# A Fourier-layer tokenizer: the second spread of each image moved from chunk 0 to chunk 3, and one relu half moved from VectorE to ScalarE

## The chip, the cores and the metric

The kernel runs on one core of a Trainium2 chip. The metric is the device time of one execution in microseconds. A core has five engines that run their own instruction streams in order and wait for each other by semaphores: TensorE (matmuls; "PE" in the profile, its weight loads "PEld"), VectorE ("DVE"), ScalarE ("ACT"), GpSimd ("POOL") and SyncE ("SP", which here issues DMAs). Matmul results land in PSUM; VectorE and ScalarE empty it.

## The reference

64 images of 256 x 256 pass a tokenizer of four Fourier layers with 32 channels, then one transformer layer. In each Fourier layer (shortened):

```python
x_ft = jnp.fft.rfft2(v)
out1 = jnp.einsum('bixy,ioxy->boxy', x_ft[:, :, :M1, :M2], W1)
out2 = jnp.einsum('bixy,ioxy->boxy', x_ft[:, :, -M1:, :M2], W2)
...
x1 = jnp.fft.irfft2(out_ft, s=(Sx, Sy))
x2 = jnp.einsum('bcxy,cd->bdxy', v, w_w[i]) + w_b[i][None, :, None, None]
v = x1 + x2
v = (v - mean) * jax.lax.rsqrt(var + BN_EPS)
v = v * bn_g[i][None, :, None, None] + bn_b[i][None, :, None, None]
if i < L - 1:
    v = jax.nn.relu(v)
```

Only 24 x 12 modes are kept (M1 = M2 = 12), so the transforms are products with small tables of sines and cosines. After the fourth layer the channels are summed to one, 77 text tokens are appended, and attention and a token-selecting feed-forward follow. All data is float32.

## The kernel before, in words

The mixing of modes (`mix`) is a small stage before each layer. The bulk is `layer(i, ...)`, run for i = 0, 1, 2: it turns mixed modes back into an image, adds the 1 x 1 product of the layer's input, applies relu, writes the new image to DRAM, and in the same pass takes the modes of the new image for the next layer. Four calls of it matter here, each a step of an image b (of 64) or of a chunk t (of 8, one eighth of an image: 128 partitions x 2048 values, 1 MB):

- `spread(b, h)`: modes to half-transformed rows, for the half h of the image (chunks 0 to 3 need h = 0, chunks 4 to 7 need h = 1). Four matmul instructions (L598) into one PSUM tile, and a VectorE transpose (L602) into `y0` or `y1`, each of which exists once. It reads `ams[b % 2]`, the image's modes, which `load_am` (L567, two DMAs on SP) brings and `scale_am` (L586, GpSimd) scales.
- `pre(b, t)`: the layer's output for one chunk. Matmuls with `y` (L616, 16 instructions), and for i > 0 with the input chunk `vin` (L627, 32 instructions), into two PSUM tiles. Relu empties the first tile on ScalarE (L634) and the second on VectorE (L635) into `vo`, and SP issues the store (L636). In layer 0 the input image itself is in the operand `mv`, so there is no L627.
- `product(b, t)`: the next layer's 1 x 1 product of the chunk (L655), squared and summed on ScalarE (L662), for the batch statistics. `turn(b, t)`: a VectorE transpose of the chunk (L643, 2.3 us, after both relu halves).
- `along_y(b)` and `along_x(b)`: the modes of the finished image. `along_y` is 256 matmuls on the turned chunks (L672), its two PSUM tiles emptied by a ScalarE copy (L682) and two VectorE transposes (L684); `along_x` is 24 matmuls (L697), a ScalarE copy (L704) and a store.

PSUM is a ring ("ring" in the profile) of four tiles of two banks, taken in the order of the calls: `pre`, `product` and `along_y` take two tiles, `spread` and `along_x` one. A call waits until the tile four takings back is emptied.

The order of the work is the order in the program, for every engine; no scheduler changes it. In the loop (L718 on) chunk t of image b runs `pre(b, t)`, the load of the input chunk four ahead, `product` of the chunk before, then in some chunks a spread, then `turn(b, t)`. In chunks 1 and 2 the products are held back; at the end of chunk 2 comes `along_y(b - 1)` and then the two held products, and at the end of chunk 3 `along_x(b - 1)`. The modes' products of the previous image are thus made inside chunks 2 and 3 of the next. `spread(b, 1)` stands in chunk 0 with `load_am(b + 2)` behind it, `spread(b + 1, 0)` in chunk 5, `scale_am(b + 2)` in chunk 6. So the order on TensorE around the change is: pre(0), product(7 of the image before), spread(b, 1), pre(1), pre(2), along_y(b - 1), product(0), product(1), pre(3), product(2), along_x(b - 1), pre(4). On VectorE: relu(0), the spread's transpose, turn(0), relu(1), turn(1), relu(2), turn(2), the transposes of along_y, relu(3), turn(3), relu(4).

Of the kernel before, what the change touches and what calls it, by code (L numbers as in the profile page):

```python
# [10 lines left out]
AF = mybir.ActivationFunctionType  # L11
ALU = mybir.AluOpType
# [123 lines left out]
def tile_fno_fusion_transformer(ctx: ExitStack, tc: tile.TileContext, a, cst_d, grid_d, out):  # L136
    nc = tc.nc
    x = a["x"].rearrange("b x y o -> b x (y o)")
    B = x.shape[0]
# [368 lines left out]
    def layer(i, st, src, dst, acc):  # L508
# [7 lines left out]
        with ExitStack() as cx:  # L516
# [48 lines left out]
            def load_am(b):  # L565
                for n in range(2):
                    nc.sync.dma_start(  # L567
                        ams[b % 2][64 * n:64 * n + 2 * KX],
                        mix_d[i][b].rearrange("p k c -> (p k) c")[:, 512 * n:512 * n + 512],
                    )  # L570

            def load_x(b):
                for n in range(4):
                    nc.sync.dma_start(
                        mv[b % 2][32 * n + 24:32 * n + 28],
                        x[b].rearrange("(j n s) y -> n j s y", j=4, n=4)[n],
                    )

            def load_v(b, t):
                vin[b, t] = ip.tile([128, 8, S], F32, name="vin")  # L580
                nc.sync.dma_start(vin[b, t], src[b][:, t])

            def scale_am(b):
                for _, p0, cs in halves:
                    v = ams[b % 2][p0:p0 + 2 * KX].rearrange("p (c k) -> p c k", k=32)
                    nc.gpsimd.tensor_tensor(  # L586
                        v, v,
                        s_[p0:p0 + 2 * KX, cs].rearrange("p (c o) -> p c o", o=1)
                        .to_broadcast([2 * KX, 16, 32]), ALU.mult,
                    )  # L590

            def spread(b, h):

                y_[b, h] = yp.tile([128, 32, C], F32, name=f"y{h}")
                ps = pp.tile([128, 2, 512], F32, name="ring")
                for n in range(2):
                    hv = slice(64 * n, 64 * n + rows_)
                    nc.tensor.matmul(  # L598
                        ps[:, n, :], lhsT=EX[hv, 128 * h:128 * h + 128], rhs=ams[b % 2][hv],
                        start=True, stop=True, skip_group_check=True,  # L600
                    )
                nc.vector.transpose(  # L602
                    y_[b, h].rearrange("p q c -> p c q"), ps.rearrange("p n (c k) -> p (n c) k", k=32)
                )

            def four():

                t2 = [pp.tile([128, 2, 512], F32, name="ring") for _ in range(2)]
                return t2, [t2[n // 2][:, n % 2] for n in range(4)]

            def pre(b, t):
                t2, ps = four()
                for r in range(2):
                    for n in range(4):
                        q = 8 * (t % 4) + 4 * r
                        nc.tensor.matmul(  # L616
                            ps[n][:, 256 * r:256 * r + 256],
                            lhsT=y_[b, t // 4][32 * n:32 * n + K, q:q + 4, :].rearrange("p q c -> p (q c)"),
                            rhs=mv[b % 2][32 * n:32 * n + K, 2 * t + r, :] if i == 0 else T4[32 * n:32 * n + K, :],
                            start=r == 0, stop=i == 0, skip_group_check=True,  # L620
                        )
                if i:
                    v = vin.pop((b, t))
                    for k in range(4):
                        for n in range(4):
                            j = (n + k) % 4
                            nc.tensor.matmul(  # L627
                                ps[n][32 * j:32 * j + 32], lhsT=ws[32 * n:32 * n + 32],
                                rhs=v[32 * n:32 * n + 32, 2 * j:2 * j + 2, :], start=False, stop=True,
                                skip_group_check=True, tile_position=(32 * n, 32 * j),  # L630
                            )
                o = vo[b, t] = op.tile([128, 8, S], F32, name="vo")
                of = o.rearrange("p (n r) y -> p n (r y)", r=2)
                nc.scalar.activation(of[:, 0:2], t2[0], AF.Relu)  # L634
                nc.vector.tensor_scalar(of[:, 2:4], t2[1], 0.0, None, ALU.max)  # L635
                nc.sync.dma_start(dst[b][:, t], o)  # L636

            def turn(b, t):

                o = vo[b, t]  # L640
                if t % 2 == 0:
                    t32[b, t // 2] = tp.tile([128, 8, 16, C], F32, name="t32")
                nc.vector.transpose(  # L643
                    t32[b, t // 2][:, :, 8 * (t % 2):8 * (t % 2) + 8, :].rearrange("p y s c -> p s y c"),
                    o.rearrange("p s (y l) -> p s y l", l=32),
                )

            def product(b, t):

                o = vo.pop((b, t))  # L650
                t2, ps = four()
                for k in range(4):
                    for n in range(4):
                        j = (n + k) % 4
                        nc.tensor.matmul(  # L655
                            ps[n][32 * j:32 * j + 32], lhsT=w4[i + 1][32 * n:32 * n + 32],
                            rhs=o[32 * n:32 * n + 32, 2 * j:2 * j + 2, :], start=True, stop=True,
                            skip_group_check=True, tile_position=(32 * n, 32 * j),
                        )
                for n in range(2):  # L660
                    at = 2 * (8 * b + t) + n
                    nc.scalar.activation(t2[n], t2[n], AF.Square, accum_out=acc[:, at:at + 1])  # L662
# [3 lines left out]
            def along_y(b):  # L666
                t2, ps = four()
                for k in range(8):
                    for m in range(4):
                        for n in range(4):  # L670
                            j = (n + m) % 4
                            nc.tensor.matmul(  # L672
                                ps[n][32 * j:32 * j + 32], lhsT=FYT[32 * n:32 * n + 32, k, :],
                                rhs=t32[b, j][32 * n:32 * n + 32, k].rearrange("p s c -> p (s c)"),
                                start=k == 0, stop=k == 7, skip_group_check=True,
                                tile_position=(32 * n, 32 * j),
                            )
                for j in range(4):
                    t32.pop((b, j))
                zt = zts[b] = zp.tile([128, 2, 32, C], F32, name="zt")  # L680
                half = zp.tile([128, 2, 512], F32, name="half")
                nc.scalar.copy(half, t2[1])  # L682
                for h, s2 in enumerate((t2[0], half)):
                    nc.vector.transpose(  # L684
                        zt[:, h].rearrange("p k c -> p c k"),
                        s2.rearrange("p n (s c) -> p c (n s)", c=C),
                    )
# [29 lines left out]
            for b in range(B):  # L717
                for t in range(8):  # L718
                    pre(b, t)
                    nb, nt = (b, t + 4) if t < 4 else (b + 1, t - 4)  # L720
                    if i and nb < B:
                        load_v(nb, nt)
                    hold = b > 0 and t in (1, 2)
                    if not hold and (b or t):
                        product(*((b, t - 1) if t else (b - 1, 7)))
                    if t == 0:
                        spread(b, 1)
                        if b + 2 < B:
                            load_am(b + 2)
                    if t == 5 and b + 1 < B:  # L730
                        spread(b + 1, 0)
                    turn(b, t)
                    if hold and t == 2:

                        along_y(b - 1)
                        product(b, 0)
                        product(b, 1)
                    if b and t == 3:
                        along_x(b - 1)
                    if i == 0 and t == 0 and b + 1 < B:  # L740
                        load_x(b + 1)
                    if t == 6 and b + 2 < B:
                        scale_am(b + 2)
            product(B - 1, 7)
            along_y(B - 1)
# [409 lines left out]
```

## Time and profile before

| | |
|---|---|
| median of three runs | 12268.8 us (12255.74 to 12290.38) |
| the profiled execution | 12259.26 us, span of its instructions 12257.5 us |
| matmuls, busy | 11179.4 us, 91% of the span |
| VectorE busy | 8789.2 us, 72% |
| ScalarE busy | 6293.1 us, 51% |
| transposes of chunks (L643) | 1536 of 2302 ns |
| relu on VectorE (L635) | 1536 of 1206 ns |
| relu on ScalarE (L634) | 1536 of 1023 ns |
| squares on ScalarE (L662) | 3072 of 1012 ns |
| DMA rate inside layer 0 (400 to 2900 us) | 207 GB/s |
| DMA rate inside layer 1 (3200 to 6000 us) | 349 GB/s |

A line of the profile's table of groups names the line of the kernel, the engine, the operation, what it writes and reads (`out<-in`), and how often. In the timeline a line begins with the start and the duration in us; brackets give the engine's idle time before it and the instruction that ended that idle time. A waits line reads: engine and line that waited, what it waited for, total us, times, longest. Matmuls of small tiles overlap each other, so a group's matmul durations add up to more than its busy time. "issue" stands for idle time for which the profile shows no wait.

### The profile page before, as it was taken

The page shows a single profiled execution, that of the slowest core. Times are in us where ns is not written, and L with a number is a line of the kernel's source. Part 1 is how long each engine was busy: PE and PEld are TensorE (multiplying, and loading weights), DVE is VectorE, ACT ScalarE, POOL GpSimd, SP SyncE. Part 2 cuts the span into 40 slices and gives each one's busy share as a digit, 9 for nine tenths or more (in the row PEclk, how much of TensorE's full clock was granted, in tenths as well). Part 3 has the DMA queues.
Part 4 walks back from the last instruction along what each step waited for, and adds up shares of the span by engine and source line. Part 5 has one row for each costly group of instructions (what it writes and reads, how often), then busy time and mean ns, then how long its engine had stood idle before and what let it go on. Part 6 is the DMA issues. An engine that isn't in the chain of part 4 may idle for free. (4 is left out here: it accounts for less than half of the span.)

```text
span 12257.5 us, 405386 instructions
## 1 busy us (share of the span) xinstructions
PE 11179.4 (91%) x182038; PEld 5979.9 (49%) x182038; DVE 8789.2 (72%) x10661; ACT 6293.1 (51%) x10441; POOL 1326.8 (11%) x1987
## 2 busy tenths in 40 slices
PE   6999999997899999999969999999999699999998
PEld 3444444444444444444434444444444466666666
DVE  6888788776777777777767777777777566666665
ACT  5666565555555555555545555555555333333333
POOL 0000000001000000000010000000000133333333
PEclk7999999998899999999989999999999799999999
DMA  7555555556988999998889999999999755555553
GB/s 224 208 209 208 202 210 208 204 205 213 343 339 346 352 352 352 353 353 347 347 305 350 350 352 353 353 350 357 349 348 349 256 217 231 229 217 233 227 218 152
DMA packets 589288, 3485.10 MB, mean 284 GB/s; under 512 B 95001, under 2 KB 144537, under 8 KB 188569
## 3 DMA queue, kind: packets, MB, share of 16 engines
q1 hardware_dynamic: 539520, 3392.84, 71.9%
q0 software_dynamic: 40880, 62.59, 2.0%
q8 instruction: 1424, 23.33, 0.8%
q10 hardware_dynamic: 7144, 3.72, 0.1%
q14 instruction: 320, 2.61, 0.1%
HBM read 1761.87 MB, written 1696.92 MB: 282 GB/s over the span
## 5 line engine op out<-in xcount | busy, mean ns | idle before, releaser
L643 DVE STREAM_TRANSPOSE t<-vo 128x2048 f32<-128x2048 f32 x1536 | 3536.3, 2302 | 162.4 <-ACT vo L634 43.6
L662 ACT ACTIVATE ring<-ring 128x1024 f32<-128x1024 f32 x3072 | 3109.0, 1012 | 504.7 <-PE ring L655 434.7
L655 PE MATMUL ring<-vo,w 32*32 32x512 f32 x49152 | 2640.1, 623 | 80.4 <-issue 62.5
L635 DVE TENSOR_SCALAR vo<-ring 128x1024 f32<-128x1024 f32 x1536 | 1852.1, 1206 | 945.5 <-PE ring L627 739.3
L634 ACT ACTIVATE vo<-ring 128x1024 f32<-128x1024 f32 x1536 | 1570.6, 1023 | 1394.8 <-PE ring L627 1232.9
L672 PE MATMUL ring<-t,cst 32*32 32x512 f32 x49152 | 1996.4, 609 | 242.4 <-issue 171.2
L616 PE MATMUL ring<-cst,y 24*128 24x256 f32 x16384 | 1404.8, 405 | 171.5 <-DVE vo L635 150.8
L672 PEld LDWEIGHTS ring<-t,cst 32*32 32x32 f32 x49152 | 973.9, 103 | 1182.5 <-issue 661.4
L655 PEld LDWEIGHTS ring<-vo,w 32*32 32x32 f32 x49152 | 821.2, 105 | 1287.7 <-issue 656.6
L616 PEld LDWEIGHTS ring<-cst,y 24*128 24x128 f32 x16384 | 893.4, 185 | 1064.5 <-ACT vo L634 375.3
L586 POOL TENSOR_TENSOR ams<-ams,bns 48x512 f32<-48x512 f32 x384 | 400.8, 1044 | 8489.8 <-DMA ams<-mix 8309.5
L682 ACT COPY half<-ring 128x1024 f32<-128x1024 f32 x192 | 194.4, 1012 | 2014.1 <-PE ring L672 2014.1
L627 PE MATMUL ring<-vin,ws 32*32 32x512 f32 x32768 | 1219.7, 619 | 2.7 <-DMA vin<-v 2.7
L602 DVE STREAM_TRANSPOSE y<-ring 128x1024 f32<-128x1024 f32 x384 | 755.0, 1966 | 399.4 <-PE ring L598 399.4
L684 DVE STREAM_TRANSPOSE zt<-ring 128x1024 f32<-128x1024 f32 x192 | 374.0, 1948 | 827.8 <-PE ring L672 827.8
L616 PE MATMUL ring<-mv,y 29*128 29x256 f32 x8192 | 802.6, 421 | 133.0 <-DVE vo L635 121.4
L616 PEld LDWEIGHTS ring<-mv,y 29*128 29x128 f32 x8192 | 503.2, 193 | 598.5 <-DVE vo L635 247.2
L697 PEld LDWEIGHTS ring<-cst,zt 128*128 128x128 f32 x4608 | 535.3, 193 | 179.0 <-ACT vo L634 164.8
L662 ACT ACTIVATION_READ_ACCUMULATOR ring<-ring 128x1 f32 x3072 | 583.4, 190 | 0.0
L1104 POOL DMA_DIRECT2D out_dram<-o x1024 | 504.4, 501 | 656.2 <-DVE o L1099 627.3
L697 PE MATMUL ring<-cst,zt 128*128 128x96 f32 x4608 | 567.4, 280 | 8.7 <-DVE zt L684 8.7
L598 PE MATMUL ring<-ams,cst 49*128 49x512 f32 (+1 forms) x1536 | 457.6, 650 | 38.2 <-POOL ams L586 28.8
(366 smaller groups left out, 9638.6 us busy)
## 6 DMA issues: line engine op xcount, KB each, us to landing
v<-vo SPq DMA_DIRECT2D x1536, 1024.0 KB
vin<-v SPq DMA_DIRECT2D x1024, 1024.0 KB
ch<-v SPq DMA_DIRECT2D x512, 1024.0 KB
mix<-ob SPq DMA_DIRECT2D x96, 512.0 KB
ams<-mix SPq DMA_DIRECT2D x384, 96.0 KB
xin<-in_x_dram SPq DMA_DIRECT2D x16, 1024.0 KB
mv<-in_x_dram SPq DMA_DIRECT2D x256, 64.0 KB
out_dram<-o POOLq DMA_DIRECT2D x1024, 16.0 KB, 3.0
```

Of the source, the lines that this page charges most:

```text
L598: nc.tensor.matmul(ps[:, n, :], lhsT=EX[hv, 128 * h:128 * h + 128], rhs=ams[b % 2][hv], start=True, stop=True, skip_group_check=True,)
L602: nc.vector.transpose(y_[b, h].rearrange("p q c -> p c q"), ps.rearrange("p n (c k) -> p (n c) k", k=32))
L616: nc.tensor.matmul(ps[n][:, 256 * r:256 * r + 256], lhsT=y_[b, t // 4][32 * n:32 * n + K, q:q + 4, :].rearrange("p q c -> p (q c)"), rhs=m ...
L627: nc.tensor.matmul(ps[n][32 * j:32 * j + 32], lhsT=ws[32 * n:32 * n + 32], rhs=v[32 * n:32 * n + 32, 2 * j:2 * j + 2, :], start=False, sto ...
L634: nc.scalar.activation(of[:, 0:2], t2[0], AF.Relu)
L635: nc.vector.tensor_scalar(of[:, 2:4], t2[1], 0.0, None, ALU.max)
L643: nc.vector.transpose(t32[b, t // 2][:, :, 8 * (t % 2):8 * (t % 2) + 8, :].rearrange("p y s c -> p s y c"), o.rearrange("p s (y l) -> p s ...
L655: nc.tensor.matmul(ps[n][32 * j:32 * j + 32], lhsT=w4[i + 1][32 * n:32 * n + 32], rhs=o[32 * n:32 * n + 32, 2 * j:2 * j + 2, :], start=Tru ...
L662: nc.scalar.activation(t2[n], t2[n], AF.Square, accum_out=acc[:, at:at + 1])
L672: nc.tensor.matmul(ps[n][32 * j:32 * j + 32], lhsT=FYT[32 * n:32 * n + 32, k, :], rhs=t32[b, j][32 * n:32 * n + 32, k].rearrange("p s c -> ...
L697: nc.tensor.matmul(ps[:, 0, 96 * g:96 * g + 96], lhsT=zt[:, h, k0:k0 + 4, :].rearrange("p k c -> p (k c)"), rhs=FX[:, h, 48 * r:48 * r + 9 ...
L1104: nc.gpsimd.dma_start(out[b, 64 * n + 16 * g:64 * n + 16 * g + 16].rearrange("(p t) d -> p t d", t=2), o[32 * g + 8 * n:32 * g + 8 * n + 8 ...
```

## The change

Three edits in `layer`. The relu of the second PSUM tile goes to ScalarE in chunk 6 of every image, and in layer 0 in chunk 1 too; all other chunks keep VectorE. `spread(b, 1)`, and `load_am(b + 2)` with it, move from chunk 0 to chunk 3, where the spread stands after product(2) and ahead of turn(3) and `along_x(b - 1)`. `scale_am(b + 2)` moves from chunk 6 to chunk 7.

```diff
                 nc.scalar.activation(of[:, 0:2], t2[0], AF.Relu)
-                nc.vector.tensor_scalar(of[:, 2:4], t2[1], 0.0, None, ALU.max)
+
+                if t == 6 or i == 0 and t == 1:
+                    nc.scalar.activation(of[:, 2:4], t2[1], AF.Relu)
+                else:
+                    nc.vector.tensor_scalar(of[:, 2:4], t2[1], 0.0, None, ALU.max)
                 nc.sync.dma_start(dst[b][:, t], o)
...
-                    if t == 0:
+                    if t == 3:
                         spread(b, 1)
                         if b + 2 < B:
                             load_am(b + 2)
...
-                    if t == 6 and b + 2 < B:
+                    if t == 7 and b + 2 < B:
                         scale_am(b + 2)
```

After it the order on TensorE around that place is: pre(0), product(7 of the image before), pre(1), pre(2), along_y(b - 1), product(0), product(1), pre(3), product(2), spread(b, 1), along_x(b - 1), pre(4).

## The prediction

> **What bounds the kernel now.** The page first, for the engines and the slices:
>
> ```profile
> PE 11179.4 (91%) x182038; PEld 5979.9 (49%) x182038; DVE 8789.2 (72%) x10661; ACT 6293.1 (51%) x10441; POOL 1326.8 (11%) x1987
> ...
> DMA  7555555556988999998889999999999755555553
> ```
>
> Slices 1 to 9 are layer 0, 10 to 19 layer 1, 20 to 30 layer 2; the rest is the attention part, which the edit leaves alone. In windows inside each layer TensorE is busy for 92 to 93% (2309.66 of 2500 us, 2611.52 of 2800, 2709.14 of 2900), with DMA at 0.55 in layer 0 and 0.91 in layers 1 and 2. So the gaps of TensorE are what can be won. Who makes them is in its waits, asked for 400 to 2900 us (layer 0, 57 images by its 57 half copies, about 43.9 us each); columns are total us, times, longest:
>
> ```profile
> PE ring L616 <- DVE vo L635: 110.8, 114, 1.5
> PE ring L672 <- DVE vo L635: 63.9, 57, 1.1
> ...
> PE ring L655 <- issue: 1.7, 5, 0.7
> ```
>
> and for 3200 to 6000 us (layer 1, again 57 images, 49.1 us each; layer 2 looks the same):
>
> ```profile
> PE ring L672 <- issue: 79.1, 59, 2.6
> PE ring L616 <- DVE vo L635: 67.2, 57, 1.4
> PE ring L655 <- issue: 25.8, 19, 2.0
> ```
>
> TensorE waits for VectorE's half of the relu at pre (L616), twice an image in layer 0 and once in layer 1, and at along_y (L672); in layer 1 the latter shows in the weight loads, 44.4 us in 57. The timeline of one image of layer 1 says which chunks. VectorE:
>
> ```profile
> 5411.84 1.98 DVE L602 STREAM_TRANSPOSE y<-ring 128x1024 f32<-128x1024 f32 x1 [1.00 <-PE ring L598]
> 5413.66 2.29 DVE L643 STREAM_TRANSPOSE t<-vo 128x2048 f32<-128x2048 f32 x1
> 5415.86 1.20 DVE L635 TENSOR_SCALAR vo<-ring 128x1024 f32<-128x1024 f32 x1
> ```
>
> This is chunks 0 and 1: the transpose of the second spread (whose matmuls began at 5410.64), turn(0), relu(1); and along_y's main part waits until 5417.11 for that relu. TensorE, at chunk 7:
>
> ```profile
> 5451.19 0.70 PE L616 MATMUL ring<-cst,y 24*128 24x256 f32 x4
> 5453.11 1.13 PE L616 MATMUL ring<-cst,y 24*128 24x256 f32 x12 [1.22 <-DVE vo L635]
> ```
>
> Pre(7) stops after 4 of its 16 matmuls: the second pair of banks of pre(6) is emptied by relu(6) on VectorE, at 5451.86 to 5453.05, behind the transpose of spread(b+1, 0) and turn(5). In layer 0 both places are worse, as VectorE has no gap from chunk 5 to chunk 2 of the next image. VectorE, and then TensorE:
>
> ```profile
> 1844.59 1.92 DVE L602 STREAM_TRANSPOSE y<-ring 128x1024 f32<-128x1024 f32 x1
> 1846.38 2.25 DVE L643 STREAM_TRANSPOSE t<-vo 128x2048 f32<-128x2048 f32 x1
> 1848.57 1.17 DVE L635 TENSOR_SCALAR vo<-ring 128x1024 f32<-128x1024 f32 x1
> ```
>
> ```profile
> 1837.67 1.13 PE L616 MATMUL ring<-mv,y 29*128 29x256 f32 x12 [1.46 <-DVE vo L635]
> ...
> 1847.63 1.05 PE L672 MATMUL ring<-t,cst 32*32 32x512 f32 x4
> 1849.80 0.72 PE L672 MATMUL ring<-t,cst 32*32 32x512 f32 x16 [1.12 <-DVE vo L635]
> ```
>
> [...] pre(7) has the gap in all 57 images, and it waits for a PSUM buffer. [...] 1.02 us at L634 against 1.21 at L635. [...] where the two "issue" rows make 105/57 = 1.84 us per image. That this is fetching beside a full DMA is my reading, not shown.
>
> **The change part by part**, as times of the images above.
>
> *Chunk 6, layers 1 and 2.* ScalarE ends relu(6)'s first half at 5451.13 and is next busy with product(5)'s square, at 5451.23; the second half goes between, 1.02 us, to 5452.15. Pre(7)'s twelve start some 0.06 later, 5452.2 instead of 5453.11: 0.91 won, 0.33 of the gap stays. Behind it on ScalarE the two squares of product(5) slide by 0.92, the second to 5454.2; product(6), which needs those banks, itself now comes at 5454.15, so this costs about nothing (0.1 at most). VectorE loses 1.2 us of work, so turn(6) starts at 5452.2 and relu(7) meets pre(7)'s new end. 0.91 x 128 images = 116 us.
>
> *Spread, layers 1 and 2.* Without it pre(1) starts where the spread did, 5410.64: its banks are now pre(0)'s (the ring moves by one), emptied by ScalarE at 5410.59 and by VectorE at 5410.85, 0.5 before the matmuls get to them. Pre(1) behind a product takes 2.21 (7636.21 to 7638.42) and pre(2) 1.97 (7643.25 to 7645.22), so along_y begins at 5414.8, its main part 0.14 later, 5414.96. VectorE: turn(0) from 5410.91, relu(1) from 5413.2 to 5414.4: in time. Main part before 5417.11, so 2.15 won. At chunk 3 the spread's 1.06 (5410.64 to 5411.70) is paid between product(2) and along_x. Its bank is free with the relu(3) that along_x waits for now. Its transpose (1.2 after its matmuls start, 1.97 long) ends some 3.2 after that start; pre(4), which needs it, comes after spread and along_x, 1.06 + 2.84 = 3.9. A cover of 0.7 us: were it gone, pre(4) would wait by as much. Turn(3) is late by 2.7 behind that transpose and relu(4) would meet it just free (turn(3) before 5436.82 to 5439.1, relu(4) at 5441.79 plus 1.06). So net 2.15 - 1.06 = 1.09, say 1.0, in the 63 images a layer that have an along_y inside: 126 us.
>
> *Layer 0*, from one along_y's end (1816.09) on. Up to product(2) nothing changes. The spread starts at 1822.69 (where along_x did), its transpose at 1823.9, turn(3) at 1825.7 instead of 1822.52, relu(4) at 1827.95 instead of 1826.78, and from there VectorE and TensorE are late by 1.06 to 1.15. Then spread(b+1, 0)'s transpose at 1833.5, turn(5) at 1835.3, and no relu(6): turn(6) at 1837.5 instead of 1837.72, relu(7) at 1839.73, turn(7) 1841.02, relu(0) 1843.26 to 1844.44. ScalarE does relu(6)'s halves from 1834.6 to 1836.6, ahead of the squares of product(5), whose matmuls now end at 1836.6. No transpose of the spread stands here now; pre(1)'s second half follows relu(0) at 1844.5 and ends at 1845.6; ScalarE empties both its halves by 1847.7 (two of 1.02; on VectorE it would have been about 1848), and along_y's main part starts at 1847.8 instead of 1849.80. 2.0 us x 63 = 126 us. What was won twice (1.46 + 1.12 and the matmuls of the spread) is mostly paid back at chunk 3.
>
> *At nothing:* load_am, two issues of together 1.0 us on SP, moves with the spread. On SP it now waits for the spread of chunk 3 with along_x's store, store(4) and load(4) behind it, all of which are made later anyway. In layer 1 the load took from 5411.87 to the scaling at 5423.78, 12 us; it is needed at chunk 5 of the next image, over 40 us on. Scaling one chunk later is POOL's 2.16 us in 46 idle ones. With that cover gone the spread would stop TensorE by up to 12 us. Store 6 now waits for ScalarE alone, and earlier.
>
> *What may come back.* Layers 1 and 2 move the same bytes in 2 us less. The peak rate in a 25 us slice there is 413 GB/s against a mean of 350, so I don't take DMA as a bound. But the "issue" waits should grow; between 0 and 1.9 us (all of the gain) I take 0.3 per image, 16% of 1.84: 38 us.
>
> Sum: 116 + 126 + 126 - 38 = 330 us. Span 12257.5 - 330 = 11927.5; the profiled execution took 12259.3 (1.8 around the span), which lies 9.5 below the median of 12268.8. Against that median: about 11940.
>
> **Rivals.** (1) *Only layer 0 wins.* The waits for VectorE in layers 1 and 2 turn into waits for instructions or for loads, at 9 tenths DMA. For it: 1.84 us of issue waits there, next to none in layer 0. Against: loads are waited for only 36 us in all (weight loads at L627), and rates go to 413. 12268.8 - 126 = 12143. (2) *Slower, by the instruction stream.* TensorE's pauses at pre(7) and along_y are when its stream catches up; without them along_y and the products behind it run dry in each image. This decides where the issue waits grow by more than the gross gain, 368 us over 126 images, 2.9 us, to 4.8 us per image; at 5.5 (three times now) it is 3.66 x 126 = 461 lost, 12268.8 - 368 + 461 = 12362. Against: the longest single one is 2.6 us. (3) *Spread's move is even.* If pre(4) waits for the transpose by 1 us or more, all the move's gain in layers 1 and 2 is gone and half of layer 0's: 116 + 63 = 179, 12090.
>
> **How the numbers follow.** The forecast has 0.70, with a range of its own of 11860 (no issue growth, which gives 38 more, and 0.3 us more per image where the steps above were read a little too dear, another 42 or so) to 12030. Rival 3 has 0.10, rival 1 0.11, rival 2 0.05, and 0.04 is for a wash. The range 11860 to 12145 takes in all of forecast, 3 and 1 but tails, a little over 8 in 10. 0.3%, about 37 us, is what a measurement of this kernel tells from no change: faster 0.91, same 0.04, slower 0.05.
>
> **What would show it.** Right: no TensorE wait for L635 at along_y in any layer; the wait of pre(7) about 0.3 us and put down to ScalarE's new line; image period about 47.5 us in layers 1 and 2 and 42 in layer 0; VectorE's relu count down by 192 + 64 = 256 of 1536. Wrong: a wait of pre(4) for the spread's transpose (rival 3), "issue" rows well over 2.2 us per image (1, 2), waits for vin or stores, or a lower granted clock: 1% of it is some 84 us of TensorE's 373 in 400 over the layers.

## The result, and the profile after

The changed kernel takes 11956.81 us (median of four, 11949.38 to 11968.81) against 12273.2 us before (median of four): a ratio of 0.9743 (95% interval 0.9726 to 0.976), 316 us less. Forecast were 11940 and about 330 less. The total is right; its parts are not: two errors of opposite sign hide in it, and that they nearly cancel is luck. The page of the profiled execution (11961.02 us):

```profile
PE 11022.9 (92%) x182038; PEld 5966.9 (50%) x182038; DVE 8507.8 (71%) x10405; ACT 6492.7 (54%) x10697; POOL 1327.1 (11%) x1987
```

VectorE has 256 instructions fewer and ScalarE 256 more, as counted. The table that tells more is by layer. It is from the half copies of the modes (L682 before, L686 after), one per image: the time from the first to the last of a layer, 63 images, and in layer 0 the shortest image (the first and the last left out).

| | layer 0 | shortest image | layer 1 | layer 2 |
|---|---|---|---|---|
| before | 2742.8 us | 42.06 | 3087.3 | 3068.2 |
| changed | 2559.5 (-183) | 40.12 | 3019.7 (-68) | 3023.2 (-45) |
| forecast of the change | -126 | -2.0 | about -102 | about -102 |

Layer 0 gave more than forecast, layers 1 and 2 half. TensorE's waits in layer 1, asked for the same stretch as before the change, 3200 to 6000 us (58 images):

```profile
PE ring L676 <- issue: 102.3, 83, 4.4
PE ring L627 <- DMA vin<-v: 27.6, 38, 1.6
PE ring L659 <- issue: 26.9, 22, 1.8
PE ring L616 <- ACT vo L637: 12.4, 58, 0.2
```

Every wait for VectorE's relu is gone, at pre and at along_y. So it is in layer 0, where the longest sums from 400 to 2700 us are short waits for ScalarE's squares, in 57 images:

```profile
PE ring L616 <- ACT ring L666: 20.0, 62, 0.3
PE ring L659 <- ACT ring L666: 16.1, 58, 0.6
```

What is left at pre(7) in layer 1 is 0.21 us an image for ScalarE's new line (0.33 forecast). But "issue" at along_y, 79.1 us before, is 102.3, and there is a wait for input chunks, 0.48 us an image, that was not there. (Line numbers from L635 on are shifted by the edit: L655, L672 and L635 before are L659, L676 and L639 now.)

The step with the thin cover, chunk 3, in one image of layer 1; TensorE, then VectorE:

```profile
4436.82 1.13 PE L598 MATMUL ring<-ams,cst 49*128 49x512 f32 x4
4437.87 2.92 PE L701 MATMUL ring<-cst,zt 128*128 128x96 f32 x24
4440.72 1.15 PE L616 MATMUL ring<-cst,y 24*128 24x256 f32 x16
```

```profile
4438.02 1.97 DVE L602 STREAM_TRANSPOSE y<-ring 128x1024 f32<-128x1024 f32 x1 [0.99 <-PE ring L598]
```

The spread's transpose ends at 4439.99, and pre(4) starts at 4440.72 without a wait: 0.73 us of cover, 0.7 in the forecast. Rival 3 is out.

### The profile page after: what moved, and what is told of

It reads as the page before. It is cut to its first block, busy times and chain, and to the rows that moved or that the text cites. A ratio compares the mean times of both kernels' runs of the same rounds, so it can differ in the third digit from the quotient of the medians.

```text
span 11959.2 us, 405306 instructions
## 1 busy us (share of the span) xinstructions
PE 11022.9 (92%) x182038; PEld 5966.9 (50%) x182038; DVE 8507.8 (71%) x10405; ACT 6492.7 (54%) x10697; POOL 1327.1 (11%) x1987
## 5 line engine op out<-in xcount | busy, mean ns | idle before, releaser
L659 PE MATMUL ring<-vo,w 32*32 32x512 f32 x49152 | 2671.7, 603 | 97.6 <-issue 61.4
L676 PE MATMUL ring<-t,cst 32*32 32x512 f32 x49152 | 1868.1, 599 | 224.6 <-issue 223.9
L639 DVE TENSOR_SCALAR vo<-ring 128x1024 f32<-128x1024 f32 x1280 | 1550.0, 1211 | 611.4 <-PE ring L627 523.2
L676 PEld LDWEIGHTS ring<-t,cst 32*32 32x32 f32 x49152 | 981.9, 103 | 1036.4 <-issue 648.1
L659 PEld LDWEIGHTS ring<-vo,w 32*32 32x32 f32 x49152 | 823.0, 103 | 1348.0 <-issue 612.6
L686 ACT COPY half<-ring 128x1024 f32<-128x1024 f32 x192 | 194.3, 1012 | 1812.9 <-PE ring L676 1812.9
L616 PE MATMUL ring<-mv,y 29*128 29x256 f32 x8192 | 746.2, 408 | 44.1 <-ACT ring L666 22.0
L616 PEld LDWEIGHTS ring<-mv,y 29*128 29x128 f32 x8192 | 465.9, 185 | 474.4 <-ACT vo L634 167.2
```

What stands on the lines that cost most here:

```text
L616: nc.tensor.matmul(ps[n][:, 256 * r:256 * r + 256], lhsT=y_[b, t // 4][32 * n:32 * n + K, q:q + 4, :].rearrange("p q c -> p (q c)"), rhs=m ...
L659: nc.tensor.matmul(ps[n][32 * j:32 * j + 32], lhsT=w4[i + 1][32 * n:32 * n + 32], rhs=o[32 * n:32 * n + 32, 2 * j:2 * j + 2, :], start=Tru ...
L676: nc.tensor.matmul(ps[n][32 * j:32 * j + 32], lhsT=FYT[32 * n:32 * n + 32, k, :], rhs=t32[b, j][32 * n:32 * n + 32, k].rearrange("p s c -> ...
```

## The experiments

On the two edits there were two theories. A: the walk through VectorE's queue that the forecast made. B: each edit wins its own wait and the two add up. On what took the gain back in layers 1 and 2, D: DMA traffic; E: nothing was there to win; and, after the first runs, F: TensorE uses up its instructions faster than they arrive, and a pause lets them catch up.

### One edit at a time

The relu edits alone:

```diff
-                    if t == 3:
+                    if t == 0:
                         spread(b, 1)
...
-                    if t == 7 and b + 2 < B:
+                    if t == 6 and b + 2 < B:
```

> The kernel before with the relu halves of chunk 6 (all layers) and chunk 1 (layer 0) on ScalarE; the spread and its loads stay at chunk 0. Theory A, by the steps of the prediction: in layer 0 VectorE is the bound from chunk 5 to along_y, and each relu half taken from it is a gain of 1.2 to 1.3 us there. Relu(6) gone brings turn(6) to relu(0) forward by 1.29, relu(1) gone takes turn(0) and relu(1) out of along_y's way: its main part at about 1846.8 in the image of the forecast against 1849.80, 3.0 us, more than the 2.0 of the whole change, as nothing is paid at chunk 3. In layers 1 and 2 0.9 an image before what DMA takes back, half of it after. 190 + 60 = 250 us, 12020; if TensorE's clock in layer 0 rises with it as in the whole change, another 50, 11970. Theory B, each edit wins its own wait and they add up: the relu edits bring about half of the whole change, 150 to 170 us, 12110.

The move of the spread alone:

```diff
-                if t == 6 or i == 0 and t == 1:
-                    nc.scalar.activation(of[:, 2:4], t2[1], AF.Relu)
-                else:
-                    nc.vector.tensor_scalar(of[:, 2:4], t2[1], 0.0, None, ALU.max)
+                nc.vector.tensor_scalar(of[:, 2:4], t2[1], 0.0, None, ALU.max)
```

> The kernel before with the second spread and its loads at chunk 3 and the scaling at chunk 7; all relu halves of the second tile stay on VectorE. Theory A: in layer 0 relu(6) still stands in the VectorE queue, so that along_y's main part comes at 1849.3 instead of 1849.80 in the image of the forecast, 0.5 us, 32 us in all; in layers 1 and 2 1.0 an image before what DMA takes back, half of it after, 63 us. Together about 95 us, 12180, and the wait of pre(7) for VectorE is still there in every layer. Theory B, the edits add up: 150 us, 12120.

The whole change without chunk 1:

```diff
-                if t == 6 or i == 0 and t == 1:
+                if t == 6:
```

> The changed kernel without its chunk 1 edit: in layer 0 relu(1)'s second half is on VectorE again. Theory A: with the spread gone from chunk 0, VectorE reaches relu(1) at about the time at which ScalarE would do it as its second relu; along_y's main part is late by 0.2 to 0.3 us, 13 to 19 us in all, 11972, nothing in layers 1 and 2. Theory B, the chunk 1 edit is what took the wait of 1.12 us out of along_y in layer 0: 70 us slower, 12027.

| | median us | ratio to before | layer 0 | shortest image | layer 1 | layer 2 |
|---|---|---|---|---|---|---|
| relu edits alone | 11859.27 | 0.967 (0.9655 to 0.9685) | 2504.6 (-238) | 39.10 | 3015.8 (-72) | 2994.7 (-74) |
| spread's move alone | 12207.87 | 0.9958 (0.9941 to 0.9974) | 2660.3 (-83) | 41.58 | 3087.7 (0) | 3087.3 (+19) |
| change without chunk 1 | 11964.52 | 0.9754 (0.9739 to 0.9768) | 2564.0 (-179) | 40.23 | 3020.9 (-66) | 3018.9 (-49) |

The relu edits alone are faster than the whole change: the intervals of their ratios do not touch. Once they are made, the move of the spread costs 98 us by the medians (105 against the change without chunk 1, measured beside them): 55 in layer 0, 4 in layer 1 and 29 in layer 2 by the table. Theory B is out.

In layer 0 the walk of theory A holds. For one image it said 3.0 us for the relu edits, 0.5 for the move, 2.0 for both; between the shortest images 2.96, 0.48 and 1.94 are measured. For the whole layer the relu edits' 238 us are its 190 and the 50 that it allowed for TensorE's clock (0.97 before, 1.00 with them). The move's 83 are more than its 32: the rest comes from the slower images, as the mean image was 1.48 us above the shortest before and 0.65 with the move, at a mean clock (below) of 0.97 and 0.96; why is open. The move takes a transpose out of VectorE's busiest stretch, but pays for it at chunk 3, where VectorE has work behind it too; after the relu edits the transpose at chunk 0 no longer stands in along_y's way. Chunk 1's edit is worth 4 us in the layer and 8 by the medians, too little to be told from nothing.

In layers 1 and 2 theory A fails. It let half of the relu edits' gain there be taken back, and none was: their total came 110 us or more below its 11970 to 12020. And it fails for the move, which was to win 1.0 us an image before DMA. TensorE's waits of the kernel with the move alone, 3200 to 6000 us (57 images):

```profile
PE ring L673 <- issue: 116.9, 91, 2.0
PE ring L616 <- DVE vo L636: 66.9, 56, 1.3
PE ring L656 <- issue: 26.5, 19, 2.0
PE ring L627 <- DMA vin<-v: 5.6, 18, 0.6
```

Per image of layer 1 (3200 to 5800 us, by the half copies in it; the wait at along_y is that of its weight loads), in us:

| | relu at pre(7) | VectorE's relu at along_y | issue | vin |
|---|---|---|---|---|
| before | 1.15 | 0.78 | 1.87 | 0 |
| spread's move alone | 1.18 | 0 | 2.57 | 0.09 |
| relu edits alone | 0.21 | 0.76 | 1.94 | 0.04 |
| changed | 0.21 | 0 | 2.26 | 0.48 |

The move removes the wait at along_y, 0.78, and gets 0.70 of issue and 0.09 of vin in its place: the sum stays to 0.01. Once the relu edits are made it is the same: the move removes 0.76, and gets 0.32 of issue and 0.44 of vin. Of the wait at pre(7), which the relu edits remove, next to nothing comes back.

### Is it DMA? Half of the loads

Layers 1 and 2 load only four of the eight rows of each input chunk, in the kernel before, in each edit alone and in the whole change:

```diff
-                vin[b, t] = ip.tile([128, 8, S], F32, name="vin")
-                nc.sync.dma_start(vin[b, t], src[b][:, t])
+                vin[b, t] = ip.tile([128, 4, S], F32, name="vin")
+                nc.sync.dma_start(vin[b, t], src[b][:, t, 0:4])
...
-                                rhs=v[32 * n:32 * n + 32, 2 * j:2 * j + 2, :], start=False, stop=True,
+                                rhs=v[32 * n:32 * n + 32, 2 * (j % 2):2 * (j % 2) + 2, :], start=False, stop=True,
```

> The kernel before with half of each input chunk of layers 1 and 2 loaded: four of the eight rows, which the products then use twice; everything else as before. A quarter of those layers' DMA bytes is gone (what is computed from the rows left out is not the reference's). Theory D, the issue waits of layers 1 and 2 (1.84 us an image) come from DMA: they go down to some 0.3, each of the two layers is faster by 80 to 100 us, 12080 in all. Theory E, they come with the program, whatever the DMA does: the layers stay within 20 us each.

> The same half loads, with the spread and its loads at chunk 3 and no relu half moved. Against the half-load kernel before: theory D, it was DMA that took the gain of this move in layers 1 and 2 (with full loads 0 us in layer 1 and 19 us lost in layer 2): now the move brings its 1.0 us an image, 63 us in each layer, beside 83 in layer 0, 210 us in all. Theory E, the move brings nothing in these layers in any case: 80 us in all, from layer 0.

> The same half loads, with only the relu halves of chunk 6, and of chunk 1 in layer 0, on ScalarE. Against the half-load kernel before: 238 us in layer 0 as with full loads, and in each of layers 1 and 2 0.9 to 1.15 us an image, 57 to 72: 350 to 380 us in all, by both theories.

> The same half loads in the changed kernel. Against the half-load kernel before: 183 us in layer 0; theory D, in layers 1 and 2 the two edits now add up, 1.9 to 2.1 us an image or 120 to 130 in each, 430 us in all, faster than the relu edits alone by some 60; theory E, 70 in each, 320 us in all, slower than the relu edits alone by 50.

| half loads | median us | layer 1 | layer 2 | issue in layer 1, us an image |
|---|---|---|---|---|
| kernel before | 12117.36 | 3033.3 | 2999.0 | 1.25 |
| spread's move alone | 12209.61 | 3056.5 (+23) | 3092.0 (+93) | 2.22 |
| relu edits alone | 11697.6 | 2926.3 (-107) | 2922.8 (-76) | 1.23 |
| changed | 11909.08 | 2996.1 (-37) | 2980.8 (-18) | 2.50 |

The medians are of three, six, two and two runs. The layers' columns are of the profiled executions; that of the first row was 40 us above its median and that of the second 36 below, so that the move's loss is rather larger than these columns say. TensorE's first wait for instructions in layer 1, 3200 to 5800 us, in the half-load kernel before (54 images) and with the move (53):

```profile
PE ring L672 <- issue: 47.0, 34, 2.9
```

```profile
PE ring L673 <- issue: 112.1, 77, 2.8
```

The DMA share in layer 1 falls from 0.91 to 0.75 in the kernel before, and the issue waits from 1.87 to 1.25 us an image. The move of the spread does not win its microsecond here either. It loses: the whole kernel is 92 us slower by the medians, where theory D had said 210 faster and E 80, and issue grows by 0.97 us an image. Nor do the two edits add up: the whole change brings 208 us (D said 430, E 320) and is 212 behind the relu edits alone, which bring 420 (350 to 380 forecast).

What this does not show is that DMA has no part in it. The traffic is not gone where the waits stand. In an image of layer 1 with half loads and the move, along_y begins at 4393.71, and TensorE waits in it for 2.16 us until 4399.44. Stretches of 4 us up to there (busy us of PE, PEld, DVE, ACT, POOL, then granted clock, DMA share, GB/s):

```profile
4390.00:4394.00 4.00, 4.00 (x102) 1.84 (x100) 3.84 (x3) 2.54 (x5) 0.00 (x0) 1.00 1.02 402
4394.00:4398.00 4.00, 3.29 (x96) 1.61 (x93) 3.89 (x3) 1.02 (x1) 0.00 (x0) 1.00 1.00 394
4398.00:4402.00 4.00, 2.56 (x82) 1.41 (x97) 1.18 (x1) 0.00 (x0) 0.00 (x0) 1.00 1.01 414
```

The DMA is as full there as with whole loads; the mean share of 0.73 for this kernel's layer 1 hides that. So the half loads do not decide between the theories.

### Issue waits: traffic or instructions?

First, layer 0 of the changed kernel with the DMA traffic of the others:

```diff
+            junk_d = [dram.tile([128, 8 * S], F32, name=f"junk{n}") for n in range(8)] if i == 0 else None
...
+                    if i == 0:
+                        nc.sync.dma_start(junk_d[t], grid_d[:, 0:8 * S])
```

> The changed kernel with a copy of 1 MB from DRAM to DRAM added per chunk in layer 0, which nothing waits for; layer 0 then moves about what layers 1 and 2 do. Theory D, issue waits come with DMA traffic: in layer 0 they rise from 0.1 us an image to 1 or more. Theory F, they need a dense stream of instructions first, and layer 0 has 96 matmul and weight instructions a chunk against 160: they stay below 0.4.

Measured: 12321.59 us, layer 0 at 2870.1, 311 us longer. The DMA share there is 0.98, more than in any layer of the kernel, and issue waits are 12.0 us in 50 images, 0.24 an image, where the changed kernel has 0.04. What TensorE waits for is ScalarE's relu, whose own wait is the output buffer's store. ScalarE's waits, 400 to 2700 us:

```profile
ACT vo L635 <- DMA v<-vo: 355.3, 151, 4.5
```

So in this run a DMA at 0.98 did not by itself make long issue waits. The pauses that the stores make may have let instructions catch up, though, so this is not a clean test.

Second, fewer instructions on TensorE in layers 1 and 2, with the spread at chunk 0 and at chunk 3:

```diff
-                    for k in range(4):
-                        for n in range(4):
-                            j = (n + k) % 4
-                            nc.tensor.matmul(
-                                ps[n][32 * j:32 * j + 32], lhsT=ws[32 * n:32 * n + 32],
-                                rhs=v[32 * n:32 * n + 32, 2 * j:2 * j + 2, :], start=False, stop=True,
-                                skip_group_check=True, tile_position=(32 * n, 32 * j),
-                            )
+                    for n in range(4):
+                        nc.tensor.matmul(
+                            ps[n], lhsT=ID, rhs=v[:, 2 * n:2 * n + 2, :], start=False, stop=True,
+                            skip_group_check=True,
+                        )
```

> The kernel before with the 1 x 1 product of layers 1 and 2 inside pre made by four wide matmuls with the identity instead of sixteen of 32 x 32 with the weights (so that product is left out; its place in the order and about its time stay): 16 instructions a chunk on TensorE in place of 64. Theory F, TensorE runs through its instructions faster than they come before and in along_y, which is what its issue waits are: with 384 fewer an image they go from 1.86 us an image to 0.5 or less. Theory D, it is DMA traffic alone that delays them: they stay between 1.5 and 2.2.

> The same with the spread and its loads at chunk 3, no relu half moved. Against the kernel of the wide matmuls with the spread at chunk 0: theory F, with instructions to spare the move now brings its 1.0 us an image in layers 1 and 2, 63 us in each, and issue waits do not grow by more than 0.2 us; if loads come late as in the changed kernel some of it is lost to vin, 40 in each at the least. Theory E, the move brings nothing in layers 1 and 2 in any case: within 20 us in each.

This pair did not test what it was made for. The four wide matmuls took 3.63 us to the next group where the sixteen packed ones take 0.88, so the kernels run at 14218.63 and 14128.4 us and an image of layer 1 takes 64 us. At that pace hardly any wait for VectorE is left for the move to win, and it changed layer 1 by 4 us (4035.4 to 4031.2). Issue was 0.88 us an image without the move and 0.85 with it (35.3 us in 40 images, 35.0 in 41): it did not grow. That agrees with F; it does not show it.

The traces show it, without a further run. The profile's table of DMA queues has one for instructions, whose packets are 16 KB each (23.33 MB in 1424 before). In the kernel before, and with the wide matmuls (queue, kind: packets, MB, share of 16 engines):

```profile
q8 instruction: 1424, 23.33, 0.8%
```

```profile
q8 instruction: 1232, 20.19, 0.6%
```

The wide kernel has 384 fewer instructions on TensorE in each of 128 images, 49152, and 192 packets fewer. So this is TensorE's queue, and a packet is a block of 256 (49152/192) of its instructions. The whole count agrees: 182038 matmuls and as many weight loads before are 1422.2 blocks of 256. The trace has the start and the length of each packet. In the fourteen traces TensorE has 2673 issue waits inside the three layers. Counted through all of TensorE's instructions in a trace, every one of them stands at the same place of a block of 256 (number 193 or 194), and every one ends 1.1 to 1.8 us after the end of a packet of this queue. An along_y of layer 1 with the move alone:

```profile
4398.70 3.58 PE L673 MATMUL ring<-t,cst 32*32 32x512 f32 x96
4403.80 4.46 PE L673 MATMUL ring<-t,cst 32*32 32x512 f32 x128 [1.52 <-issue]
4410.01 1.15 PE L673 MATMUL ring<-t,cst 32*32 32x512 f32 x32 [1.75 <-issue]
```

Between the two waits lie 128 matmuls, with their weight loads 256 instructions; the packets went from 4401.38 to 4402.30 and from 4407.69 to 4408.66. An issue wait of TensorE in these layers is thus a wait for the next block of its own instructions, as theory F had it.

DMA traffic makes the block late in these runs, so theory D has its part. A packet takes about 1 us (medians of 0.94 to 1.06) whatever the traffic, but it starts later. From TensorE's first instruction of one block to the start of the packet for the next, the median is 0.94 us in layer 0 and 3.33 in layer 1 of the kernel before, and 1.85 with half loads; in layer 0 of the changed kernel the added copies raise it from 0.95 to 2.66. Of the 75 issue waits from 3200 to 5800 us before, 74 stand where the DMA share around the block's start was 0.95 or more, as it was for 294 of the 383 blocks; with half loads and the move, 80 of 83, where it was so for 189 of 388.

This fits with one gain kept and the other not. In the image above it is 6.21 us from TensorE's first instruction of a block to that of the next: 3.89 to the start of the packet, 0.97 for the packet, 1.35 until TensorE goes on. The median over all blocks of layer 1 that end in an issue wait is 6.21 too, before and with the move alone. TensorE's own work in this block is 4.46. A pause in such a block is time in which the next one arrives. In the kernel before, only 5 of the 62 blocks of layer 1 in which along_y's weight loads wait for VectorE's relu end in an issue wait. Without that pause more blocks do: of 106 that begin in along_y (3200 to 5800 us), TensorE waits for 55 before and for 85 with the move alone. The blocks around pre and product last longer by themselves: with the relu edits alone 7.0 us (median) for those whose successor begins in pre, and only 5 of these 159 successors are waited for, against 56 of 110 in along_y. So the wait at pre(7) could be won. This is read from the traces; no run was made to test it.

### The load ahead of the store

In the changed kernel, then with the relu edits alone:

```diff
-                nc.sync.dma_start(dst[b][:, t], o)
...
                     if i and nb < B:
                         load_v(nb, nt)
+                    nc.sync.dma_start(dst[b][:, t], vo[b, t])
```

> The changed kernel with each chunk's load of the input four ahead issued before the store of the chunk, on the same queue, instead of behind it; nothing else. Theory A: in layers 1 and 2 part of the gain was taken back by loads that now come late (TensorE at L627 waits for vin 0.48 us an image, 0.03 before). The store waits for relu, the load for matmuls that end about 1.1 us sooner, and it no longer runs behind the store's 1 MB (2.6 us at 400 GB/s): the load lands 3 us earlier and the wait goes, 0.45 x 126 = 57 us, 11900. Theory C, the loads' wait is only where a DMA queue that is full shows, and the bytes take their time anyway: within 0.3% of the changed kernel, the wait moves to instructions (issue) or stores.

> The relu edits alone, the spread left at chunk 0, and each chunk's load issued before its store. With the spread at chunk 0 the loads were not waited for, so most of what the earlier load won in the changed kernel (78 us) is not there to win: 11859 less 0 to 30 us, 11830 to 11860. If it is the order of stores and loads itself that helps, 11790.

In the changed kernel: 11878.3 us (ratio 0.9687, 0.9672 to 0.9701), 78.5 us less than the changed kernel; layers 1 and 2 at 2989.5 and 2975.1, the wait for vin gone, layer 0 unmoved. Theory A was right on this wait; it had forecast 57 us. With the relu edits alone: 11802.21 us (ratio 0.9629, 0.9611 to 0.9647), 57 us below those edits without it, between the two expectations. There the loads were hardly waited for (0.04 us an image), so only part of it is that wait; issue waits fall too, from 1.94 to 1.63 us an image of layer 1. What the rest is stays open. This version is the fastest of all that load every row, 155 us below the changed kernel.

## Why the prediction was right, and where its parts were wrong

**Chunk 6, layers 1 and 2: 116 forecast, 145 measured** (72 + 74 with the relu edits alone). The mechanism is as told: a gap of 1.15 us an image at pre(7) becomes 0.21. ScalarE's second relu starts 0.92 us after its first, not 1.02, which is 0.1 of the 1.14 us an image. The rest of the difference to 0.91 stays open; TensorE's clock in layer 1 was 0.98 before and 0.99 with the relu edits alone.

**The spread, layers 1 and 2: 126 forecast, 38 of it lost; measured a loss of 19** (0 in layer 1). This is the step that failed. The wait at along_y was removed as said, though it was 0.78 us an image in the mean, less than the 1.0 that was taken from one image; that TensorE would then run on into along_y without another wait was wrong. With the move alone issue waits grew by 0.70 us an image where 0.3 were put in; with the whole change they grew by 0.39, near the 0.3, but vin waits came to 0.48 where none was expected. What stood in the way is the next block of TensorE's instructions, which, where it is waited for, comes 6.2 us (median) after the one before: the pause that was removed had been the time in which it arrived. The prediction's reading of the issue waits, fetching beside a full DMA, was the right one; its sum did not follow from it, as it took the DMA for no bound because of its mean rate. In the kernel before, TensorE waited for 6 of 279 packets in layer 0 (400 to 2700 us) and for 75 of 383 in layer 1 (3200 to 5800 us).

**Loads are not a bound.** Wrong by 0.48 us an image: of the 36 us of waits before, all but 2.7 were in weight loads that hid behind matmuls, but the load of chunk 2, issued behind the store of chunk 6, had no slack. In the image shown of the changed kernel it is issued at 4405.57 and awaited until 4416.32.

**Layer 0: 126 forecast, 183 measured.** The walk was good to 0.06 us for the shortest image (1.94 against 2.0). For the mean of the images that ran at full clock (20 of 61 before, 60 of 61 after; the first and the last left out) it is 42.37 less 40.64, 1.73 us, or 109 in 63 images. What came on top is a term that the sum had only as a risk: TensorE's clock. From 400 to 2700 us its mean was 0.97 before and 1.00 after. Stretches of 2 us around the wait of pre(7), 1490.2 to 1491.7, in a slow image of the kernel before (busy us of PE, PEld, DVE, ACT, POOL, then granted clock, DMA share, GB/s):

```profile
1488.00:1490.00 2.00, 2.00 (x36) 0.53 (x32) 2.00 (x2) 0.79 (x2) 0.00 (x0) 1.00 0.48 197
1490.00:1492.00 2.00, 0.54 (x8) 0.31 (x8) 1.90 (x3) 1.92 (x4) 0.00 (x0) 1.00 0.00 0
1492.00:1494.00 2.00, 2.00 (x28) 0.81 (x36) 2.00 (x2) 1.02 (x1) 0.00 (x0) 0.55 0.77 315
1494.00:1496.00 2.00, 2.00 (x40) 0.84 (x12) 1.89 (x3) 0.56 (x1) 0.00 (x0) 0.50 0.50 201
1496.00:1498.00 2.00, 2.00 (x30) 1.07 (x40) 2.00 (x2) 2.00 (x5) 0.00 (x0) 0.50 1.04 430
1498.00:1500.00 2.00, 2.00 (x36) 0.30 (x4) 0.68 (x1) 0.87 (x2) 0.00 (x0) 0.74 0.56 234
```

After a pause of 1.46 us the clock is half for 6.8 us here (1492.2 to 1499.0). In the timeline the twelve matmuls behind the pause then take 1.61 us, where they took 1.13 in the image of the forecast:

```profile
1491.68 1.61 PE L616 MATMUL ring<-mv,y 29*128 29x256 f32 x12 [1.46 <-DVE vo L635]
```

The clock fell after 27 of the 53 such pauses between 400 and 2700 us: by the trace's records of the granted clock it was 0.50 for 3.41 us after 19 of them and for 6.83 us after 8. Of 12 more falls in that stretch, 11 came within 0.4 us behind along_y's wait of 1.12 us. This is what made the layer's images uneven: those at full clock take 42.06 to 42.87 us, the 14 with a mean clock below 0.93 take 44.53 to 47.54. All 61 have a mean of 43.65, 1.28 more than those at full clock, which is 81 us in 63 images (an estimate; with the 109 it makes 190, and 183 are measured). That it is the pause at pre(7) fits the runs: the layer-0 clock is 1.00 in all runs without a wait of pre(7) for VectorE or for stores, and 0.94 to 0.97 in all with one.

**The rivals and the sum.** Rival 1 (12143) is out as a sum, since in layers 1 and 2 about half of the gross gain stayed; but its mechanism, waits for VectorE that turn into waits for instructions or loads, is what became of the spread's half. Rival 2 had the same mechanism at a far larger size. Rival 3 (12090) is out by its mechanism, as pre(4) waits for the spread's transpose only in the first image of a layer, which has no along_x; that the move would be worth nothing in layers 1 and 2 was right, for another reason. The three layers account for 296 of the 298 us between the two profiled executions; the medians are 316 apart. Against the 330 forecast, layer 0 gave 57 more, mostly through a clock that was not in the sum, and layers 1 and 2 gave 91 less: the total came out right by luck.

## What to carry to other kernels

Where an engine's queue is full, walk through that queue instruction by instruction: in layer 0 that gave each edit's effect to 0.1 us, and would have shown beforehand that one of the two edits was better alone. Where the engine whose gaps are to be closed already shows waits that nothing explains, a closed gap need not be won: look whether these waits stand at equal numbers of instructions and behind packets of the instruction queue, and test each edit alone before they are put together. A mean DMA share can hide stretches in which the DMA is full: here 0.73 hid stretches at 1.00 to 1.02. Count a load's slack from its issue to its use, not from the waits that happen to be hidden.

## What the runs showed of the hardware

- TensorE's instructions came in packets of 16 KB, 256 instructions each (49152 fewer instructions, 192 fewer packets), and TensorE stood still for one 75 times from 3200 to 5800 us in layer 1 of the kernel before, 99 us in all, 74 of them with a DMA share of 0.95 or more.
- TensorE's granted clock fell to 0.50 after 27 of 53 pauses of 1.46 us in layer 0 of the kernel before, for 3.41 us after 19 of them and for 6.83 us after 8.
- Four 128 x 128 float32 matmuls with 512 columns (eight instructions in the trace) took 3.63 us, start to next group; sixteen of 32 x 32 on the same data, packed four by four, took 0.88 (median of 1036, kernel before).
- ScalarE's second relu of 128 x 1024 in chunk 6 of the changed kernel started 0.92 us after the first, and each took 1.02: they overlapped by 0.1 us.
